# Deformable attention on one core: the weighted sum of the values as matmuls with matrices of weights, for both images at once

## The chip, the cores and the metric

The kernel runs on one core of a Trainium2 chip. The metric is the device time of one execution in microseconds (us), the median over runs. An engine is named as the profile names it: PE (matmuls) and PEld (its weight loads), DVE, ACT, POOL, and SP, which issues transfers. Transfers ("DMA") run on 16 DMA engines that all queues share; a queue belongs to the engine that issues (SP, ACT or POOL).

## The reference, cut to what matters

The program computes two layers on two images of 64 x 64 pixels with 256 channels: a deformable attention, a graph-attention mixture of experts, a windowed attention and a second mixture of experts. The change touches only the first, whose core is this, for 8 groups `g` of 32 channels and 9 sample points each:

```python
qkv = _dwconv_nhwc(x @ qkv_w + qkv_b, dw_w, dw_b)            # 1x1 and depthwise 3x3
for g in range(G):                                           # G = 8 groups, HC = 32 channels
    off = conv(q)[g] + base[g]                               # base: the 9 points of a 3x3 raster, spacing r = 2g + 1
    k_list.append(_flow_warp(k_map[:, sl], off) * mask)      # bilinear samples at y + off_y, x + off_x, clipped to the image
    v_list.append(_flow_warp(v_map[:, sl], off) * mask)
attn = softmax(einsum('bgpc,bgpkc->bgpk', q * HC ** -0.5, k))
out = einsum('bgpk,bgpkc->bgpc', attn, v)
return out @ proj_w + proj_b
```

`_flow_warp` reads the four pixels around a point with bilinear weights. Since the learned part of an offset is below one pixel on this data (the kernel tests it and has a gathering path for the other case, which does not run here), a point of group g lies within one pixel of its raster place. So each of the 9 points is a sum over a fixed 3 x 3 patch with "tent" weights, and the output of a pixel is a sum over 9 rows (`ky` = 0, 1, 2 of the raster times `sy` = 0, 1, 2 of the patch) of 9 pixels each (`kx`, `sx`), every one with a weight of its own: attention weight x mask x tent in y x tent in x.

## The kernel before, in words

Everything is float32. A pixel is named by image `b`, row `y` and column `x`; 128 partitions hold (b, y), both images' rows, unless said otherwise.

`static_maps` (L209 to L378) makes the maps in DRAM: normalisation and the 1x1 projection in 16 chunks (L236 to L259), the depthwise convolution of queries and values on DVE (L207) and of keys on PE (L349), the offsets (L365 to L378). The sorting of the graph's edges, which belongs to a later layer, is woven in (`edges`, L224, `next(edges)`). The query tile `q0` is cleared by one POOL memset (L276); `borders` (L309) has POOL issue 32 transfers that repeat the edge pixels of the value map `vd`, which is stored with 16 repeated rows and columns around each image. `qd` and `kd` are the query and key maps.

`static_attention` (L381) then works group by group, in the order 1, 2, ..., 7, 0. In phase n it weaves three lists of steps ("lanes") together by their relative place in each list: `group_values` of group n, `group_weights` of group n + 1, `group_dots` of group n + 2. Two phases before the first have no values. Every engine runs its instructions in the order so written.

- `group_dots` (L440): for a half of the columns and one `kx`, PE multiplies the 64 queries of a column with the 64 x 3 keys of three columns (L473, 32 channels deep, one image at a time, four column blocks of 8 on partitions 0, 32, 64, 96; two sets of PSUM buffers), ACT copies the products to a staging tile (L480, in the first two phases DVE takes half), and ACT issues the store to `dots` in DRAM (L492).
- `group_weights` (L506): SP reads the logits back, shifted by row (`pick`, L545, pieces of 128 bytes), DVE applies the tents, the softmax and the mask (L588 to L627), POOL multiplies the last tent in (L633, nine products of 128 x 576). The result `wt[ky]` holds for each (b, y) and x the 81 weights.
- `group_values` (L682): for each of the 9 shifted rows SP loads the value map, shifted by dy, into `vt` (L711; 64 partitions per transfer, up to 11.8 KB each). ACT spreads the row's weights into PSUM (L717). Then, for each `kx` and each quarter of the columns, DVE multiplies three shifted windows of values with their weights (L733, 128 x 1536), POOL adds one or two of the three products together (L740, 128 x 512), and PE adds what is left to the accumulators with an identity matrix (L746, 128 x 512). After the last row ACT copies the four accumulators out (L756) and issues their stores to `od`.

`project_out` (L772) reads `od` back by tiles of 128 pixels, transposes them on PE, multiplies by `proj_w` and adds input and bias. Later layers follow and are the same in both kernels.

## Time and profile before

| what | value |
|---|---|
| median of 10 runs | 6117.68 us (6105.75 to 6138.07) |
| profiled execution, its own time | 6120.16 us |
| span in its profile | 6118.3 us |
| maps, `static_maps` | about 0 to 985 us |
| the two phases without values | about 985 to 1232 us |
| eight phases with values (first product to last copy out) | 1232 to 3178 us |
| first accumulator copied out (L756), phase by phase | at 1593.6, 1847.0, 2103.0, 2362.5, 2625.3, 2854.6, 3070.3 and 3143.5 us |
| projection, `project_out` | about 3180 to 3300 us |

The span is the time from the first to the last instruction; the execution's own time is 1.9 us longer, and this execution is 2.5 us above the median. In a line of a group, "x2716 | 1402.0, 662" means 2716 instructions that kept the engine busy for 1402.0 us together and took 662 ns each on average; behind the next bar stands the idle time just before them and what ended it. A float32 matmul appears as two matmul instructions, each with its own weight load; a transpose appears as one. PEclk is the granted clock of PE, 1.0 being full. DMA share is the mean busy share of the 16 DMA engines.

### The profile page before, as it was taken

Reading aid. Unit: us, or ns where it says so; the run is one execution under the profiler, and the core shown is the slowest. Engines: PE = TensorE matmul, PEld = TensorE weight load, DVE = VectorE, ACT = ScalarE, POOL = GpSimd, SP = SyncE. Lnnn points to the kernel's source line nnn. Section 1 sums busy time; section 2 is a strip of 40 time slices with the busy share of each in tenths; the row PEclk is TensorE's granted clock in tenths of the full one; section 3 lists DMA queues with packets and bytes.
Section 4 is the critical chain, followed back from the end, with each engine's and each line's share of the span. In section 5 each row is a group of like instructions: output and inputs, shape, how many; then the busy total and the mean of one; then the engine's idle time right before and its main releaser. Section 6 shows DMA issues by size and latency. Waiting matters only on the chain. (4 is left out here: it accounts for less than half of the span.)

```text
span 6118.3 us, 68586 instructions
## 1 busy us (share of the span) xinstructions
PE 4977.6 (81%) x23911; PEld 2992.5 (49%) x23911; DVE 3728.1 (61%) x6085; ACT 1441.6 (24%) x2580; POOL 2270.7 (37%) x1994
## 2 busy tenths in 40 slices
PE   9999985597998988999878586089977878869993
PEld 5645784333343433343335243068853444448882
DVE  7897766375888888899955577011136555542223
ACT  3222111223333323321003000022223444412220
POOL 0000000054787877788841773700025111110016
PEclk9989986566988979899889798599987888879996
DMA  5436667534545546564243200277742000038885
GB/s 163 147 111 157 133 54 128 121 99 106 132 128 128 146 123 154 124 147 99 58 95 73 12 6 3 99 229 224 224 141 79 21 21 21 21 127 267 265 269 182
DMA packets 946767, 740.49 MB, mean 121 GB/s; under 512 B 611794, under 2 KB 833246, under 8 KB 935264
## 3 DMA queue, kind: packets, MB, share of 16 engines
q1 hardware_dynamic: 725004, 488.35, 31.9%
q10 hardware_dynamic: 185812, 167.81, 10.2%
q0 software_dynamic: 35584, 79.71, 4.4%
q8 instruction: 197, 3.23, 0.2%
q14 instruction: 170, 1.39, 0.1%
HBM read 469.87 MB, written 276.15 MB: 122 GB/s over the span
## 5 line engine op out<-in xcount | busy, mean ns | idle before, releaser
L746 PE MATMUL acc<-prod,ident 128*128 128x512 f32 x2716 | 1402.0, 662 | 154.6 <-POOL prod L740 131.5
L733 DVE TENSOR_TENSOR prod<-vt,wp 128x1536 f32<-128x1536 f32 (+1 forms) x796 | 1334.8, 1732 | 219.3 <-PE acc L746 163.3
L740 POOL TENSOR_TENSOR prod<-prod 128x512 f32<-128x512 f32 x1010 | 1307.8, 1319 | 428.7 <-DVE prod L733 402.3
L746 PEld LDWEIGHTS acc<-prod,ident 128*128 128x128 f32 x2716 | 527.7, 206 | 828.0 <-issue 555.2
L480 ACT COPY stage<-dot 128x384 f32<-128x384 f32 (+1 forms) x640 | 482.6, 840 | 1084.7 <-PE dot L473 909.0
L473 PE MATMUL dot<-kt,qt 32*64 32x192 f32 (+1 forms) x5888 | 516.4, 419 | 152.6 <-ACT stage L480 85.2
L1501 PE MATMUL ps_h<-xgT,w1t 128*128 128x256 f32 x2240 | 540.0, 388 | 31.1 <-DVE xgT L1496 24.6
L473 PEld LDWEIGHTS dot<-kt,qt 32*64 32x64 f32 x5888 | 282.2, 166 | 547.0 <-ACT stage L480 269.5
L1509 PE MATMUL ps_y<-w2t,hT 128*128 128x256 f32 x2240 | 507.4, 380 | 0.0
L1512 DVE TENSOR_TENSOR y<-ps_y,b2t 128x256 f32<-128x256 f32 x280 | 118.8, 424 | 627.2 <-PE ps_y L1509 458.2
L1501 PEld LDWEIGHTS ps_h<-xgT,w1t 128*128 128x128 f32 x2240 | 414.9, 192 | 110.2 <-DVE xgT L1496 34.3
L1509 PEld LDWEIGHTS ps_y<-w2t,hT 128*128 128x128 f32 x2240 | 426.5, 190 | 58.3
L1504 ACT ACTIVATE hT<-ps_h,b1t 128x256 f32<-128x256 f32 x560 | 259.1, 474 | 814.9 <-PE ps_h L1501 778.0
L1234 PE MATMUL ps<-oh,ol 128*128 128x512 f32 (+1 forms) x864 | 327.4, 542 | 95.1 <-DVE oh L1227 95.1
L2127 POOL DMA_INDIRECT xs<-tn,sloti x128 | 124.8, 975 | 610.5 <-DVE slot L2125 521.4
L1596 POOL DMA_INDIRECT back<-ys,back_row x128 | 124.9, 976 | 583.1 <-DVE run L2112 538.2
L207 DVE SCALAR_TENSOR_TENSOR cv<-pad,colt,cv 128x2048 f32<-128x2048 f32 x128 | 296.4, 2340 | 0.0
L1234 PEld LDWEIGHTS ps<-oh,ol 128*128 128x128 f32 x864 | 169.9, 198 | 252.3 <-issue 210.2
L349 PE MATMUL ps_k<-padk,diag 128*128 128x512 f32 x576 | 269.7, 623 | 19.6 <-ACT km L354 19.3
L1494 PE MATMUL ps_x<-ident,xg 128*128 128x128 f32 x560 | 84.9, 275 | 217.3 <-DMA xg<-xs 217.3
L1118 PE MATMUL psc<-oh,ol 128*128 128x64 bf16 x1792 | 239.1, 305 | 21.9 <-DVE oh L1116 21.9
L1118 PEld LDWEIGHTS <-ol 128*128 128x128 bf16 x1792 | 225.2, 148 | 52.8 <-issue 40.7
(392 smaller groups left out, 5968.8 us busy)
## 6 DMA issues: line engine op xcount, KB each, us to landing
w1t<-in_W SPq DMA_DIRECT2D x140, 512.0 KB
w2t<-in_W SPq DMA_DIRECT2D x140, 512.0 KB
xg<-xs SPq DMA_DIRECT2D x140, 256.0 KB
ys<-y ACTq DMA_DIRECT2D x140, 256.0 KB
kt<-kd SPq DMA_DIRECT2D x176, 160.0 KB
pr<-stage SPq DMA_DIRECT2D x16, 1584.0 KB
pad<-pr SPq DMA_DIRECT2D x16, 1122.0 KB
b2t<-in_b SPq DMA_DIRECT2D x140, 128.0 KB
```

The lines of the kernel that those rows point to most:

```text
L207: nc.vector.scalar_tensor_tensor(out, src, w, out, ALU.mult, ALU.add)
L349: nc.tensor.matmul(ps.rearrange("p a b -> p (a b)"), lhsT=diag[:, tap, :], rhs=pad[:, at : at + 8, tap % 3 : tap % 3 + W], start=(tap == 0 ...
L473: nc.tensor.matmul(ps[jj][H * b : H * b + H, i, 0 : m * H], lhsT=qt[at, i0 + i, :, b], rhs=kt[at, i0 + i : i0 + i + m, b, :], start=True, ...
L480: (nc.vector.tensor_copy if alone and jj else nc.scalar.copy)(box["d"][:, 0:m, :, x : x + 2].rearrange("p s y i -> p i (s y)"), ps[jj][:, ...
L733: nc.vector.tensor_tensor(pr[:, 0:m], win, wp[:, xh, 0:m, XQ * xq : XQ * xq + XQ].unsqueeze(3).to_broadcast([P, m, XQ, HC]), ALU.mult,)
L740: nc.gpsimd.tensor_tensor(pf[:, 0], pf[:, 0], pf[:, s], ALU.add)
L746: nc.tensor.matmul(box["a"][i].rearrange("p x c -> p (x c)"), lhsT=self.ident, rhs=pf[:, s, :], start=i not in started, stop=last,)
L1118: nc.tensor.matmul(psc, lhsT=ol[:, :, j], rhs=oh[:, :, j], start=(c1 == 0), stop=(c1 == NW - 1),)
L1234: nc.tensor.matmul(psf[:, c : c + m], lhsT=ol, rhs=ohf[:, c : c + m], start=(start and j == 0), stop=(stop and j == n - 1),)
L1501: nc.tensor.matmul(ps, lhsT=w1t[:, k, f * P : (f + 1) * P], rhs=xT[:, k, :], start=(k == 0), stop=(k == CC - 1),)
L1504: nc.scalar.activation(hT[:, f, :], ps, AF.Gelu, bias=b1t[:, f : f + 1])
L1509: nc.tensor.matmul(ps, lhsT=hT[:, f, i * P : (i + 1) * P], rhs=w2t[:, f, :], start=(f == 0), stop=(f == NF - 1),)
```

## The change

The sum over rows is rewritten as a matmul over the rows of both images. For a column x of the output, a half `h` of the columns and one `kx`, a matrix `[ (b, y source), y output ]` holds the weights; times the values of one column, `[ (b, y source), (b, channel) ]`, it gives the output column. The value tile has, for each (b, y), 32 channels in its own image's place and zeros in the other's, so one matmul sums both images without mixing them.

- **Zeros.** The matrices `wd[g]` lie in DRAM (`[H, B, 6, H, 3, XH]`: source row, image, (kx, h), output row, column shift, column). They are mostly zero. `zeros()` has POOL write them during `static_maps`, from a zero tile of 16 partitions in pieces of 1536 bytes, only inside the band of rows that a band of 16 source rows can reach (`band`): 368 transfers, 74.5 MB in all, eight in flight. `some(n, after)` issues n portions, behind a small POOL copy that waits for ACT's or DVE's current tile. 192 transfers (33.0 MB) stand ahead of the memset of `q0` on POOL.
- **Weights.** `along_x` is cut into three products of 128 x 192 per (ky, sy). Rows outside the image are added to the edge row's weights (`fold`, eight DVE operations of 128 x 576 per group, for g = 0 four), so the map needs no repeated rows. SP writes the nine weight rows onto the diagonals of `wd[g]` (`write`), in pieces of 384 bytes.
- **Values.** `value_map` loads a group's values once (two pieces), DVE copies them into `vt`, four copies a group. For each of 6 runs (h, kx) POOL issues eight transfers of 16 partitions that load the matrix into one of two tiles `mats`. PE then does 240 float32 matmuls a group (128 rows deep, 64 columns wide, up to 192 long, moving operand read with a step of 384 bytes), in pairs on the two halves of the output partitions. `clear` zeroes the accumulators by matmuls, `end` has ACT copy them out.
- **Dots.** Both images in one matmul: queries are loaded twice and masked by DVE (`own`), 64 channels deep, 128 wide, 192 long; half as many matmul instructions. Four sets of PSUM buffers instead of two; queries in one buffer instead of two; the store goes by bands of 16 rows in long runs, and `pick` reads pieces of 384 bytes.
- **Projection.** `od` is stored by channel, so `project_out` loads eight pieces of 32 partitions and needs no transposes; its matmuls take 64 pixels each.

The diff at its core:

```diff
+ORDER = list(range(1, G)) + [0]
+BAND = 16
+def band(g, y):
+    r = 2 * (g or G - 1) + 1
+    return max(0, y - r - 1) // 4 * 4, min(H, (y + BAND + r + 1 + 3) // 4 * 4)
...
@@ static_maps
+            zero = zp.tile([P, 4 * 3 * XH], F32, name="zero")
+            nc.gpsimd.memset(zero, 0.0)
+            def zeros():
+                for g in ORDER:
+                    for y in range(0, H, BAND):
+                        lo, hi = band(g, y)
+                        for b in range(B):
+                            for k in (range(6) if g else (0, 1, 4, 5)):
+                                to = wd[g][y : y + BAND, b, k, lo:hi].rearrange("y (n f) s x -> y n (f s x)", f=4)
+                                ins = nc.gpsimd.dma_start(
+                                    to, zero[0:BAND].unsqueeze(1).to_broadcast([BAND, (hi - lo) // 4, 4 * 3 * XH])
+                                )
+                            yield
+            def some(n, after=None):
+                if after is not None:
+                    nc.gpsimd.tensor_copy(tick, after)
+                for _ in range(n):
+                    next(fill, None)
...
+                    some(2, st[:, 5, 7, 1:2])
...
+                    some(3, cv[:, 0, 0:1])
...
+                some(B * G * H // BAND)
...
@@ static_attention
-                "prod": pool("atp", 8), "dram": pool("atd", 2, space=DRAM), "wp": pool("atw", 2, space=PSUM),
-                "dot": pool("ats", 2, space=PSUM), "acc": pool("ata", 1, space=PSUM),
+                "dram": pool("atd", 2, space=DRAM), "dot": pool("ats", 4, space=PSUM), "acc": pool("ata", 1, space=PSUM),
+            mats = [pools["one"].tile([P, H, 3, XH], F32, name=f"mat{i}") for i in range(2)]
+            pools["vt"] = pools["one"].tile([P, W + 2 * BORDER, B, HC], F32, name="vt")
...
@@ group_dots
+            box["q"] = qt = pools["one"].tile([P, XQ, H, B], F32, name="qt")
+            nc.vector.tensor_tensor(qf, qf, own.unsqueeze(1).to_broadcast([P, XQ * H, B]), ALU.mult)
...
+            for i in range(2):
+                for jj in range(2):
+                    at = slice(64 * jj, 64 * jj + 64)
+                    nc.tensor.matmul(
+                        ps[jj][:, i, :], lhsT=qt[at, i0 + i].rearrange("p y b -> p (y b)"),
+                        rhs=kt[at, i0 + i : i0 + i + 3, :].rearrange("p s y -> p (s y)"), start=True, stop=True,
+                    )
...
@@ group_weights
+            for sx in range(3):
+                nc.gpsimd.tensor_tensor(
+                    wt[ky][:, sy, :, 2 - sx, :], halves(t5[:, sx, 0, 3 * ky : 3 * ky + 3, :]),
+                    halves(box["wy"][:, sy]), ALU.mult,
+                )
...
+        def fold(i, to):
+            nc.vector.scalar_tensor_tensor(a, weights(i), edge[:, m : m + 1], a, ALU.mult, ALU.add)
+        def write(i):
...
+                        ins = nc.sync.dma_start(
+                            dst, weights(i)[H * b + lo : H * b + hi, k : k + n].rearrange("p k s x -> p k (s x)")
+                        )
...
@@ group_values
+        def load(n):
+            h, kx, _ = runs[n]
+            for b in range(B):
+                for y in range(0, H, BAND):
+                    lo, hi = band(g, y)
+                    nc.gpsimd.dma_start(mats[n % 2][H * b + y : H * b + y + BAND, lo:hi], wd[y : y + BAND, b, 2 * kx + h, lo:hi])
+        def add(n, j0, j1):
...
+                    for q in range(2):
+                        at = m.offset + a * XH + XQ * q + j - 2 + a
+                        nc.tensor.matmul(
+                            sums[h][64 * q : 64 * q + 64, j - 2 + a : j - 2 + c, :].rearrange("p x y -> p (x y)"),
+                            lhsT=vt[:, r + 1 + XH * h + XQ * q + j + dx].rearrange("p b c -> p (b c)"),
+                            rhs=bass.AP(m.tensor, at, [m.ap[0], [XH + 1, c - a], [3 * XH, H]]),
+                            start=False, stop=last and (j, a) == over,
+                        )
+        steps.append(value_map)
+        steps.append(lambda: load(0))
+        steps.append(lambda: load(1))
+        for n, (h, kx, dx) in enumerate(runs):
+            if n % (len(runs) // 2) == 0:
+                steps.append(lambda h=h: clear(h))
+            for j in range(0, XQ + 2, 3):
+                steps.append(lambda n=n, j=j: add(n, j, j + 3))
+            if n + 2 < len(runs):
+                steps.append(lambda n=n: load(n + 2))
+            if (n + 1) % (len(runs) // 2) == 0:
+                steps.append(lambda h=h: end(h))
```

## The prediction, made before the changed kernel ran

> **What bounds the kernel now.** I read the granted clock and span first (one core, clock 0.853), then the busy table by 40 slices, then busy times cut at the stage boundaries, then the costliest groups and the waits of the stage that changes. The sums over stages:
>
> ```profile
> core 0: us, PE busy (x) PEld busy (x) DVE busy (x) ACT busy (x) POOL busy (x), PEclk, DMA share, GB/s
> 0.00:320.00 320.00, 301.93 (x1376) 196.78 (x1377) 250.92 (x777) 94.43 (x163) 7.49 (x10) 0.94 0.47 155
> 320.00:985.00 665.00, 597.47 (x3074) 443.48 (x3073) 540.41 (x695) 107.97 (x113) 23.00 (x19) 0.91 0.60 105
> 985.00:1232.00 247.00, 135.18 (x1136) 77.41 (x1136) 112.62 (x179) 59.23 (x75) 13.85 (x18) 0.50 0.59 144
> 1232.00:1620.00 388.00, 343.10 (x1620) 147.50 (x1620) 259.77 (x188) 112.04 (x169) 232.90 (x179) 0.74 0.48 114
> 1620.00:2855.00 1235.00, 1132.02 (x5296) 475.52 (x5296) 1049.34 (x692) 381.03 (x603) 968.06 (x748) 0.89 0.55 131
> 2855.00:3180.00 325.00, 270.33 (x575) 111.35 (x568) 272.79 (x186) 21.74 (x53) 220.73 (x200) 0.92 0.34 69
> 3180.00:3300.00 120.00, 83.87 (x384) 65.45 (x384) 83.89 (x296) 26.42 (x84) 32.25 (x17) 0.88 0.60 149
> ```
>
> From 1620 to 2855 us PE is busy 92%, DVE 85%, POOL 78%, and the transfers a little over half. The three busy engines work on one chain, as the page's groups show:
>
> ```profile
> L746 PE MATMUL acc<-prod,ident 128*128 128x512 f32 x2716 | 1402.0, 662 | 154.6 <-POOL prod L740 131.5
> L733 DVE TENSOR_TENSOR prod<-vt,wp 128x1536 f32<-128x1536 f32 (+1 forms) x796 | 1334.8, 1732 | 219.3 <-PE acc L746 163.3
> L740 POOL TENSOR_TENSOR prod<-prod 128x512 f32<-128x512 f32 x1010 | 1307.8, 1319 | 428.7 <-DVE prod L733 402.3
> ```
>
> The product on DVE, the sum on POOL and the identity matmul wait for one another in turn; each alone fills two thirds of the 1946 us between the first product (1232) and the last copy out (3178). A phase lasts 252 us (first copies out at 1593.6 and 2854.6, five phases apart). The copies and reductions that remain are in the same stretch (1232 to 3180 us, shapes kept apart):
>
> ```profile
> L480 ACT COPY stage<-dot 128x384 f32<-128x384 f32 x539 | 411.1, 855 | 837.7 <-PE dot L473 719.5 <-DMA dots<-stage 53.1 <-PE acc L746 21.9
> L756 ACT COPY o<-acc 128x512 f32<-128x512 f32 x32 | 18.8, 587 | 115.7 <-PE acc L746 48.7 <-DMA lk<-dots 33.0 <-DMA od<-o 19.8
> ...
> L613 DVE TENSOR_REDUCE red<-lg 128x64 f32<-128x576 f32 x7 | 8.0, 1143 | 0.2
> L612 DVE TENSOR_TENSOR lg<-lg,mask 128x576 f32<-128x576 f32 x7 | 5.5, 785 | 0.2
> ```
>
> L480 writes with a step of 128 bytes and takes 2.2 ns an element, L756 without a step 1.15; L613 reads with a step of 256 bytes and takes 2.0 ns, L612 without 1.36. A step costs up to a factor of two.
>
> **The change, per phase of groups 1 to 7.** What goes: L733, L740, L746 and the spreading copy L717 (73.3 us on ACT): 1335 us of DVE, 1308 of POOL and 1402 of PE. What then sets the phase? I bill every engine.
>
> PE. Dots: 48 steps a group. A step was 16 instructions, of which four ran side by side, in 0.87 to 0.88 us at full clock (timeline near 1612 us); now it is 8, two side by side, so again four rounds of 192 columns: 48 x 0.87 = 42 us. Values: 36,864 columns on two halves that run side by side as the dots' tiles do, so 18,432, in two instructions, at 0.84 ns (a round of 192 columns started 162 ns after the last): 31 us if the step of 384 bytes is free, 62 us at the factor of two above, 124 us if the two halves also share the reads. I take 62, the nearest row. Clearing: 4 matmuls of 512 columns, 4 us. Sum 108 us (79 to 170); PE is in order, so a late matrix also holds the dots behind it.
>
> ACT. 96 copies x 0.855 = 82 us (the step becomes 384 bytes; L480 already pays), 24 stores at 0.82 us of issuing = 20, copies out and tents 10: 112 us.
>
> DVE. All but L733 and L480 is 240 us in seven phases, 34 us each; eight folds at 0.8 (128 x 576), two masks of 2048 elements at 2.4 (twice the 1.22 us of 128x1024), four value copies of at most 1.7, smaller pieces 2: 54 us. POOL: 27 products at a third of 1.5 us, 16 us, and 48 issues at 0.5 to 1.15 us (the border transfers): 40 to 71 us. SP: about 118 transfers at 0.52 to 0.62 us: 68 us. None of these binds.
>
> Transfers, in us of all 16 engines, from the packets in the trace: dots stores 9.1 MB at 16.8 bytes/ns (5632 bytes in 336 ns) 34; keys 768 x 4608 bytes 13; queries, twice as many, 7; values, loaded once, 4 (before: nine loads, 48); logits read and weights written, 6912 pieces each at 23 ns (256 bytes took 18, 512 took 27) 20; offsets and output 6. That is 84. The matrices, 9.5 MB, come by 16 partitions, which no row shows: 27 us at the rate of a 128-partition load (8976 bytes in 410 ns), 35 at that of the 32-partition dots stores, and at most 108 if a quarter of the first rate is left, since 64-partition value loads had already dropped to 11,776 bytes in 844 ns. I take 50, between the two nearer values because 16 partitions are fewer than any row. Sum 134 (111 to 192). The busiest slices of the page show 8 tenths; at 0.84 the phase is 134 / 0.84 = 160 us. This is the largest bill, so **160 us a phase**, 132 to 256 at the ends (192 at 0.75).
>
> [...]
>
> Waits between phases. The first matrix of a group waits for the last products (POOL), folds (DVE), 12 writes (SP, behind whose waits the next keys queue) and their landing: 3 x 0.6 + 4 x 0.8 + 12 x 0.55 + about 5 = 17 us, then the load. POOL issues these last products after the load that waits for run 3 of 6, so two runs of PE, some 50 us, cover it. Without that cover it would cost 17 to 30 us a phase.
>
> Group 0 has four runs and no dots beside them: 4 x 18 us of load and matmul and 18 us to the end, 90 us, against 110 before.
>
> Stage: 7 x 160 + 90 = 1210 instead of 1946: **-736 us**.
>
> **The rest.** Zeros: 74.5 MB in 48,512 pieces of 1536 bytes beside the maps. Before, 0 to 985 us holds 549 us of all DMA engines (0.47 x 320 + 0.60 x 665). At 70 ns a piece (between 1024 bytes at 54 and 2048 at 97) the zeros add 212: 761 of 985, hidden, with PE at 90% setting the pace. At a quarter of that rate they add 850, and the maps grow by up to 414 us. On POOL 368 issues cost under 420 us, off the path, but the clearing of q0 (at 324.5 us before) now follows 192 of them, 33 MB: ACT's copies into q0, and after two tiles DVE, wait for it. I take +40 (0 to +250, since the engines seldom stand on the same pieces). The two phases without values: PE no longer waits for single PSUM pairs, but the weights of group 1 still follow dots, softmax and now writes and a load: 0 (-60 to +20). Projection: 128 transposes go (20.6 us), yet all eight loads and the input (16.8 MB, 67 us at 250 GB/s) stand before the first matmul, where before they ran beside: +15 (-15 to +60).
>
> Sum on the profiled execution's 6120: 6120 - 736 + 40 + 15 = 5439, **5440 us**; the median, 2.5 us lower, makes no difference to that.
>
> **The rivals.** Written by T, the time of a phase: 6120 - 1946 + 90 + 55 + 7T = 4319 + 7T.
>
> - All transfers at their low ends. T = 111 / 0.84 = 132, with ACT's 112 and PE's 108 just below: 5243 us. For it: 32-partition loads run at 17 bytes/ns. Against: three engines near the same bill seldom overlap fully.
> - The matmuls become the bound: the two halves share the strided reads, and dots run at the 0.74 clock of 1232 to 1620 us: 124 + 57 + 4 = 185, with waits for matrices 200: 5719 us. For it: ACT's and DVE's rows at half rate. Against: the dots' tiles lose nothing side by side.
> - Slower: transfers by 16 partitions run at a quarter. T = 256, the maps +250 instead of +40: 4319 + 1792 + 210 = 6321 us. It decides where T passes 257 with cheap zeros, or 227 with dear ones. For it: the drop from 128 to 64 partitions. [...]
>
> **How the numbers follow.** Forecast (5300 to 5650) 0.53, first rival 0.17, second 0.22, slower one 0.06; the rest, 0.02, is a wait between phases that cancels the gain or leaves no change. The range runs from below the first rival to above the second, 5190 to 5780, and leaves out a little under 2 in 10. Under 0.2% either way (about what this measurement can tell) is next to impossible between such values: 0.01. Faster 0.92, slower 0.07.
>
> **What would show it.** Right: L733, L740, L717 gone; first copies out 140 to 190 us apart; DMA share 0.75 or more there, with DVE and POOL under half. The value matmuls at about 320 ns instead of 160 a round show the step's price; 640 the second rival. Matrix loads much longer than 20 us, with PE waiting for them, show the 16-partition price. A q0 memset far after 324 us, or the start of dots far after 985 us, shows the zeros' cost. The prediction is wrong if phases stay above 230 us or the maps grow by more than 200.

## The result and the profile after

The changed kernel takes 6321.14 us (median of 8 runs, 6307.59 to 6336.02) where the kernel before takes 6119.88 (28 runs): 1.0329 times as long, 95% interval 1.0318 to 1.0341. The forecast was 5440, range 5190 to 5780. It is slower by 201 us, and the forecast had the wrong sign.

The two profiled executions have spans of 6308.2 and 6118.3 us, 189.9 apart. Cut at the same four events (first dots matmul, first instruction on values, last copy out, end) they give the whole difference:

| stretch | before, us | after, us | difference | forecast |
|---|---|---|---|---|
| maps: 0 to the first dots matmul | 995.0 | 1680.3 | +685.3 | +40 (0 to +250) |
| dots and weights alone, to the first instruction on values | 237.4 | 238.5 | +1.1 | 0 |
| stage with values, to the end of the last copy out | 1946.3 | 1431.6 | -514.7 | -736 |
| the rest | 2939.6 | 2957.8 | +18.2 | +15 |

This is the table of busy times of the changed kernel, in stretches that end with the chunk loop (739), the first dots matmul (1680.3), the first value matmul (1918.8) and the last copy out (3350.4):

```profile
core 0: us, PE busy (x) PEld busy (x) DVE busy (x) ACT busy (x) POOL busy (x), PEclk, DMA share, GB/s
0.00:739.00 739.00, 492.01 (x2482) 345.01 (x2482) 511.46 (x1403) 93.08 (x162) 104.03 (x197) 0.72 0.58 106
739.00:1680.30 941.30, 463.69 (x1984) 307.00 (x1985) 317.90 (x146) 107.13 (x114) 156.46 (x229) 0.74 0.89 127
1680.30:1918.80 238.50, 115.70 (x742) 97.52 (x742) 115.31 (x146) 72.54 (x92) 26.24 (x44) 0.68 0.49 128
1918.80:3350.40 1431.60, 886.41 (x5949) 601.29 (x5948) 308.68 (x382) 408.87 (x589) 304.02 (x565) 0.78 0.75 150
3350.40:6308.20 2957.80, 2177.86 (x10969) 1534.51 (x10969) 1237.42 (x3371) 642.63 (x1344) 801.30 (x823) 0.84 0.41 121
```

The chunk loop ended at 289 us before and ends at 739. Through it PE is busy 67% of the time (94% in the first 320 us before), DVE 69% and the DMA engines 58%: nothing is full. From 739 to 1680 the share is 0.89. In the stage with values, where PE, DVE and POOL were all busy before, PE is down to 62%, ACT to 29%, DVE to 22%, POOL to 21%, and the DMA engines stand at 0.75. So the old bound is gone, and none of the bills has taken its place in full.

The page's groups, which answer to the three (L746, L733, L740) and to L480 of before:

```profile
L534 PE MATMUL dot<-kt,qt 64*128 64x192 f32 x2944 | 473.5, 417 | 646.5 <-DVE qt L518 240.9
...
L541 ACT COPY stage<-dot 128x384 f32<-128x384 f32 x640 | 444.6, 853 | 861.8 <-PE dot L534 466.0
L847 PE MATMUL acc<-mat,vt 128*64 128x192 f32 (+2 forms) x3680 | 499.7, 439 | 121.9 <-DMA mat<-wd 121.9
...
L825 POOL DMA_DIRECT2D mat<-wd x368 | 179.7, 494 | 911.0 <-PE acc L847 533.4
...
L259 POOL DMA_DIRECT2D wd<-zero x368 | 197.3, 540 | 347.3 <-DMA wd<-zero 330.0
```

The value matmuls (L847) cost 500 us where product, sum and identity matmul cost 1335, 1308 and 1402 on their three engines. A copy of dots costs 853 ns, 855 before. New are 911 us in which GpSimd waits at L825 ahead of a matrix load, 533 of them for value matmuls to leave a buffer, and 330 us in which it waits for earlier zeros before it can issue more (L259).

What holds the chunk loop shows in the waits from its 45th us to its end (columns: total us, times, longest), first of the changed kernel, then of the kernel before:

```profile
engine line waited for: us in total, times, longest us
POOL tick L272 <- ACT stage L306: 528.8, 14, 62.5
ACT stage L306 <- PE ps_q L302: 248.7, 70, 24.1
ACT stage L306 <- DMA pr<-stage: 245.5, 7, 45.2
```

```profile
ACT stage L255 <- PE ps_q L251: 154.5, 89, 6.4
```

Before, ACT's copies into the staging buffer waited only for PE, at most 6.4 us at a time. Now they wait seven times, up to 45 us and 245 in all, for the store of a chunk to leave the buffer that they want to refill; they also wait 94 us more for PE. The store hasn't changed: 1584 KB in packets of 2112 bytes, whose median is 88 ns. What is new beside it are the zeros' packets: 14,208 of 4608 bytes, median 739 ns, 6.2 bytes/ns. All the zeros' packets add up to 717 us of all 16 engines.

At the end the dots wait for the zeros themselves. The last offset copy starts at 1531.7 us (954.1 before), and PE then stands from 1564.3 to 1680.3, until DVE has masked the queries:

```profile
DVE qt L518 <- DMA mask<-offd: 87.2, 1, 87.2
```

The view names the loads of the sample mask, but these are issued only at 1675.9, behind the load of `edge` (L449), which holds the mask for the queries. SyncE stands from 1600.2 to 1675.4 before it issues that load, and the profile puts this down to the zeros, whose last packet ends at 1674.9. So 578 of the 685 us lie ahead of the last offset copy, and some 75 of the rest are a plain wait for the last zero.

In the stage the copies out end at 2034.6, 2300.7, 2488.3, 2705.5, 2914.7, 3141.9, 3273.3 and 3350.4 us, one group each: 188 to 266 us apart while dots run beside, 131 for group 7, 77 for group 0, on the average (3273.3 - 1918.8) / 7 = 193.5 us instead of 160.

### The profile page after: what moved, and what is told of

Same layout as the page of the kernel before. It is cut to its first block, busy times and chain, and to the rows that moved or that the text cites. A ratio compares the mean times of both kernels' runs of the same rounds, so it can differ in the third digit from the quotient of the medians.

```text
span 6308.2 us, 63605 instructions
## 1 busy us (share of the span) xinstructions
PE 4135.7 (66%) x22123; PEld 2885.3 (46%) x22123; DVE 2490.8 (39%) x5448; ACT 1324.2 (21%) x2300; POOL 1392.0 (22%) x1856
## 5 line engine op out<-in xcount | busy, mean ns | idle before, releaser
L534 PE MATMUL dot<-kt,qt 64*128 64x192 f32 x2944 | 473.5, 417 | 646.5 <-DVE qt L518 240.9
L534 PEld LDWEIGHTS dot<-kt,qt 64*128 64x128 f32 x2944 | 378.1, 233 | 751.0 <-issue 523.0
L541 ACT COPY stage<-dot 128x384 f32<-128x384 f32 x640 | 444.6, 853 | 861.8 <-PE dot L534 466.0
L847 PE MATMUL acc<-mat,vt 128*64 128x192 f32 (+2 forms) x3680 | 499.7, 439 | 121.9 <-DMA mat<-wd 121.9
L847 PEld LDWEIGHTS acc<-mat,vt 128*64 128x64 f32 x3680 | 309.1, 159 | 309.0 <-issue 225.9
L825 POOL DMA_DIRECT2D mat<-wd x368 | 179.7, 494 | 911.0 <-PE acc L847 533.4
L302 PE MATMUL ps_q<-xT,wq 128*128 128x512 f32 x384 | 225.7, 730 | 106.5 <-ACT stage L306 94.7
L259 POOL DMA_DIRECT2D wd<-zero x368 | 197.3, 540 | 347.3 <-DMA wd<-zero 330.0
L395 PEld LDWEIGHTS ps_k<-padk,diag 128*128 128x128 f32 x576 | 114.5, 202 | 336.3 <-issue 211.5
## 6 DMA issues: line engine op xcount, KB each, us to landing
mat<-wd POOLq DMA_DIRECT2D x112, 192.0 KB, 12.4
```

The costliest lines, as they stand in the source:

```text
L259: ins = nc.gpsimd.dma_start(to, zero[0:BAND].unsqueeze(1).to_broadcast([BAND, (hi - lo) // 4, 4 * 3 * XH]))
L302: nc.tensor.matmul(ps.rearrange("p a b -> p (a b)"), lhsT=wq[:, k, c * P : (c + 1) * P], rhs=xT[:, k, :], start=(k == 0), stop=(k == CC - 1),)
L395: nc.tensor.matmul(ps.rearrange("p a b -> p (a b)"), lhsT=diag[:, tap, :], rhs=pad[:, at : at + 8, tap % 3 : tap % 3 + W], start=(tap == 0 ...
L534: nc.tensor.matmul(ps[jj][:, i, :], lhsT=qt[at, i0 + i].rearrange("p y b -> p (y b)"), rhs=kt[at, i0 + i : i0 + i + 3, :].rearrange("p s y ...
L541: (nc.vector.tensor_copy if alone and jj else nc.scalar.copy)(box["d"][:, :, :, x : x + 2].rearrange("p y s i -> p i s y"), ps[jj].rearran ...
L847: nc.tensor.matmul(sums[h][64 * q : 64 * q + 64, j - 2 + a : j - 2 + c, :].rearrange("p x y -> p (x y)"), lhsT=vt[:, r + 1 + XH * h + XQ * ...
```

## The experiments

Two questions: what made the maps 685 us longer, and why a phase takes 194 instead of 160 us. For the first, theory A is the 16-partition source of the zeros, theory B their place in GpSimd's order, theory C its queue. For the second, theory M (transfers set the phase) stands against W (waits in a chain), and later S (SyncE's in-order queue).

Experiments 9 to 12, 17 and 18 ran on two chips where the kernel before takes 6116 to 6118 us, the others on three where it takes 6400 to 6411, so ratios are to the kernel before on the same chip. The 280 us between these chips lie behind the last copy out (2954 to 2963 us there on the first two, 3238 to 3252 on the other three); where an edit left the maps alone they end at the same time on all, so lengths of maps and stage can be compared across.

### 1. Zeros from 96 partitions

```
-  for b in range(B):
-      for k in (range(6) if g else (0, 1, 4, 5)):
-          to = wd[g][y : y + BAND, b, k, lo:hi] ...            # from zero[0:BAND]
+  for h in range(2):
+      to = wd[g][y + 8 * h : y + 8 * h + 8, :, :, lo:hi].rearrange("y b k (n f) s x -> (y b k) n (f s x)", f=4)
+      nc.gpsimd.dma_start(to, zero[0:96] ...)
```

> The changed kernel, but each strip's zeros leave 96 partitions in two transfers instead of 16 partitions in twelve; same queue, same places in GpSimd's order, 3.9 MB more (group 0 gets all six blocks). Theory A (the 16-partition source is slow, 4608 bytes in 739 ns, and other transfers wait behind its packets): packets of 4608 bytes fall to 180-290 ns, the zeros' engine time from 23% of the span to under 10%, the first dots matmul comes at 1000-1150 us instead of 1680, total 5640-5790. Theory B (the zeros' place in GpSimd's order holds up the sort and the clearing of q0): the maps keep most of their 685 us, total 6100-6300.

Measured: 0.9585 of before (0.9557 to 0.9613). The table of busy times up to the end of the chunk loop, to the first dots matmul, and in the stage:

```profile
core 0: us, PE busy (x) PEld busy (x) DVE busy (x) ACT busy (x) POOL busy (x), PEclk, DMA share, GB/s
0.00:493.00 493.00, 315.40 (x1262) 192.09 (x1262) 241.40 (x753) 92.65 (x162) 60.53 (x86) 0.74 0.74 224
493.00:1232.10 739.10, 608.04 (x3216) 454.61 (x3214) 586.88 (x796) 108.18 (x114) 47.94 (x35) 0.87 0.63 122
...
1467.80:2891.70 1423.90, 889.24 (x5949) 606.78 (x5948) 308.48 (x382) 408.35 (x589) 307.06 (x565) 0.78 0.75 151
```

The first dots matmul comes at 1232.1 instead of 1680.3, 448 us earlier, and the stage is as before (1424 instead of 1432). The packets of 4608 bytes fall from a median of 739 ns to 178 (mean 254), the zeros' engine time from 717 to 271 us. Of the 448 us, 335 lie ahead of the last offset copy (1531.7 to 1197.1) and 113 behind it, since the last zero now lands at 553 and nothing waits for it. One thing in the expectation doesn't hold: a step of the filling now covers both images, so all strips, not half, are issued beside the chunks (the DMA rate there is 224 GB/s). Theory A gets most of the loss, but less than it said (dots at 1000 to 1150); 237 us remain. The edit also makes 64 transfers out of 368; experiment 4, which changes the partitions of a load and not the number of loads, shows that the partitions alone can make packets shorter (12288 bytes in 834 ns instead of 1362).

### 2. The same zeros issued by SyncE

```
-  ins = nc.gpsimd.dma_start(to, zero[0:BAND] ...)
+  ins = nc.sync.dma_start(to, zero[0:BAND] ...)
```

> The changed kernel, with the same 368 transfers of zeros from 16 partitions issued by SyncE instead of GpSimd. Theory A: the packets stay at 739 ns, the maps stay within 100 us of 1680, total 6200-6450. Theory B, or a theory C (GpSimd's software queue itself is slow): packets at 200-300 ns or a chunk loop that ends near 290 us, total 5650-5900.

Measured: 1.0859 (1.0837 to 1.0882). The table (columns as before) up to the end of the chunk loop and to the first dots matmul:

```profile
0.00:627.00 627.00, 303.50 (x1088) 177.51 (x1089) 204.73 (x621) 96.67 (x162) 11.95 (x26) 0.70 0.63 115
627.00:2033.50 1406.50, 633.05 (x3387) 478.37 (x3386) 630.97 (x929) 109.91 (x114) 39.67 (x30) 0.66 0.57 88
```

The rate stays: 1536 bytes in 232 ns is 6.6 bytes/ns, and the packets add up to 634 us. The maps take 353 us longer still, against the 100 expected. The chunk loop ends earlier than in the changed kernel (627 for 739), but the convolution of the keys comes later: its loads stand behind the zeros in SyncE's queue. The last zeros are issued at 1630.8 and the first of these loads at 1632.8 (788.3 in the changed kernel); the convolution runs from 1641 to 1897 us (804 to 1324). Theory C falls. So does B for the clearing of q0: without zeros on GpSimd it comes 47 us after the chunk loop; in the changed kernel it comes 51 after it, before the change 36. The loop is late, not the clearing.

### 3. Two buffers for the queries

```
-  qt = pools["one"].tile(...)           # and raw of 48 columns, o of 16
+  qt = pools["first"].tile(...)         # two buffers; raw of 12 columns, o of 4 to make room
```

> The changed kernel with two buffers for the queries qt instead of one (room comes from value_map in pieces of 12 columns and copies out in quarters). Theory W (a phase of some 205 us is a chain of waits, and PE, ACT and GpSimd all stand while the one qt is filled and masked, two gaps of 25 to 30 us a phase): first copies out 150-175 us apart, total 6030-6130. Theory M (the transfers set the phase): under 60 us gained, total 6260-6330.

Measured: 1.0529 (1.0512 to 1.0547), the stage 1575 us instead of 1432. This says nothing on the queries alone: the values now come in up to eight pieces through one small buffer, and DVE waits 108 us for these pieces. Experiment 7 asks the question without that.

### 4. Rows on every fourth partition

```
-  nc.gpsimd.dma_start(mats[n % 2][H * b + y : H * b + y + BAND, lo:hi], wd[...])
+  nc.gpsimd.dma_start(mats[n % 2][H * b + y // BAND : H * b + H : H // BAND, lo:hi], wd[...])
```

> The changed kernel with the rows of a strip laid on every fourth partition of 64 instead of on 16 neighbours, for the matrices and the values alike, so that each matrix load reaches 64 partitions' width with the same bytes (the values come in eight loads instead of one). Theory M (matrix packets of 12288 bytes at 1336 ns set the phase): packets near 700 ns, phases 170-180 us, total 6080-6170. Theory W: packets fall, but the phase stays within 10 us of 205, total 6250-6330.

Measured: 1.0129 (1.0103 to 1.0155), 1.9% below the changed kernel. Over the stage the median packet of 12288 bytes falls from 1362 to 834 ns, that of 18432 from 2328 to 1361. The stage (columns as before):

```profile
1921.00:3240.10 1319.10, 898.83 (x5949) 604.77 (x5948) 313.00 (x382) 408.70 (x589) 301.24 (x565) 0.80 0.67 163
```

It is 1319 us long, 113 less, at a DMA share of 0.67. That lies between the two forecasts, so it decided nothing by itself.

### 5. The wide zeros, spread

```
-  some(2, st[:, 5, 7, 1:2])
+  if i8 % 2:
+      some(1, st[:, 5, 7, 1:2])
```

> The zeros of the first experiment (96 partitions, two transfers a strip), but spread: one strip after every second chunk and three after each tile of values, so that 8 of 32 strips lie beside the chunks instead of all 32. If the first experiment's remaining 237 us (dots at 1232 instead of 995) are its 64.7 MB crowded beside the chunks, the chunk loop ends at 295-350 us, the first dots matmul comes at 1010-1090, ratio to the kernel before 0.92-0.945. If zeros cost their bytes wherever they lie, the dots stay at 1180 or later and the ratio at 0.95-0.96.

Measured: 0.9598 (0.9575 to 0.9622), the same as experiment 1. The chunk loop ends at 401 us instead of 493 and the last offset copy comes at 1111 instead of 1198, but the dots at 1209. The edit did less than it says: a zero transfer doesn't depend on the copy that paces it, and in GpSimd's order transfers stand ahead of these copies (12 of 64 before the first), so some 53 of 78 MB still moved before 400 us.

### 6. Spread zeros, every fourth partition, two query buffers

```
-  qt = pools["one"].tile(...)           # values through raw and nc.vector.tensor_copy
+  qt = pools["first"].tile(...)
+  nc.gpsimd.dma_start(vt[H * b + y // BAND : H * b + H : H // BAND, 0:wb, b, :], vd[g, b, y : y + BAND, ...])
```

> The experiment before it, with every strip's rows on each fourth partition (as in the fourth experiment, both images' loads in turn), two buffers for the queries, the values loaded by GpSimd straight into vt (no raw tile, no copies on VectorE) and the copies out in halves. Theory M (transfers set the phase): the fourth experiment's 112 us of the stage and little more, ratio 0.90-0.925. Theory W (the waits for queries and values stand in the chain as well): phases of 150-180 us, 150 us more, ratio 0.875-0.90.

Measured: 0.9413 (0.9392 to 0.9434), outside both ranges: the maps take 1179 us instead of the 1010 to 1090 on which both counted, and the stage 1343, more than with experiment 4 alone. Two query buffers with values that GpSimd writes straight into vt bring nothing.

### 7. Half the queries' refills left out

```
   def queries(h):
+      if h:
+          return
```

> The changed kernel without the second half's queries (the first half's, already masked, are used again, so the second half's dot products are left out of the reference's sum), which takes away one of the two refills of qt a phase and nothing else. Theory W: each refill stops PE, ACT and the matrix loads for 25-40 us, so 7 x 25-40 = 175-280 us less than the changed kernel, ratio to the kernel before 0.99-1.006. Theory M: under 60 us less, ratio 1.023-1.033.

Measured: 1.0268 (1.0248 to 1.0288), 0.6% or some 39 us below the changed kernel, the stage 1406. That is M's side: the refill of qt in the middle of a phase is worth 4 to 6 us. In the changed kernel PE shows gaps of 4 to 14 us at these refills; those at a phase's start, with gaps of up to 28 us, stayed, and no run leaves them out.

### 8. Value matmuls that read neighbours

```
-  rhs=bass.AP(m.tensor, at, [m.ap[0], [XH + 1, c - a], [3 * XH, H]])
+  rhs=bass.AP(m.tensor, at, [m.ap[0], [H, c - a], [1, H]])
```

> The changed kernel with the value matmuls reading 64 to 192 neighbouring elements instead of elements 384 bytes apart (the sums are then over other weights, so the attention's output is left wrong); instructions, columns and waits are the same. If the step doubles a value matmul, as the prediction had it, L847 falls from 500 to 250-300 us of busy time. If PE is on the path, the ratio falls by that share, to 0.995-1.012; if transfers or waits set the phase it stays at 1.02-1.035. If L847 stays at 450-500, the step costs nothing.

Measured: 1.0336 (1.0317 to 1.0356), no difference. The group of the value matmuls of 192 columns, shapes kept apart, in the changed kernel and in this one (total us, mean ns):

```profile
L847 PE MATMUL acc<-mat,vt 128*64 128x192 f32 x2208 | 390.2, 502 | 0.0
```

```profile
L847 PE MATMUL acc<-mat,vt 128*64 128x192 f32 x2208 | 239.1, 364 | 0.0
```

The mean length of an instruction falls from 502 to 364 ns, but instructions overlap, so that is not the price. In the changed kernel a round of 192 columns (an instruction on each half) starts 325 ns after the last, in this one 163 (medians over the stage): the step of 384 bytes doubles a round, as the prediction had it. The busy time of L847 falls from 500 to 301 us, at the edge of what was expected for a doubling. And it gains nothing: PE isn't on the path.

### 9. Zeros for one group of eight

```
-  for g in ORDER:                        # zeros into wd[g]; matrices read wd[g]
+  for g in [G - 1]:                      # zeros into wd[G], a ninth tile; matrices read wd[G]
```

> Zeros for one group instead of eight (11.8 MB from 96 partitions into a tile of its own, where every group's matrix loads now read; the weights are still written, but nobody reads them, so the attention's output is left wrong). So far each us of engine time that zeros added (719 us in the changed kernel, 283 in the first experiment) put the first dots matmul off by 0.84 to 0.95 us. Theory M (the maps wait for transfers, even at a DMA share of 0.6): 11.8 MB are some 40 us of engine time, first dots matmul at 1025-1050 us. If ticks and order on GpSimd cost something of their own: 1090 or later. In the stage no load waits for weights to land: theory W then gives phases 20 us or more below 205, theory M within 10 us.

Measured: 0.9334 (0.9312 to 0.9356). The last offset copy starts at 970.8 us, 17 after the 954.1 of before, with 40 us of zeros. The first dots matmul comes only at 1070.8, between the two forecasts. In the last stretch ahead of it (965 to 1075 us) PE and GpSimd wait for this:

```profile
PE dot L533 <- DVE qt L517: 63.2, 1, 63.2
POOL topa L1263 <- DVE top L1261: 50.5, 1, 50.5
```

The dots now wait for the mask on qt, an instruction of DVE that the change adds, and DVE is in the middle of the edge sort then; SyncE, too, issues the loads of the queries only behind the sort's, at 1061. That is a wait of about 60 us which the late zeros of the changed kernel had hidden. The stage doesn't test W cleanly: values of a group start before its weights, its gaps are 216 to 225 us with dots beside, none shorter.

### 10. Spread zeros and every fourth partition

```
   # the edits of experiments 5 and 4, and:
-  for b in range(B):
-      for y in range(0, H, BAND):        # matrix loads
+  for y in range(0, H, BAND):
+      for b in range(B):
```

> The wide, spread zeros of the fifth experiment with the rows on every fourth partition and both images' loads in turn; one qt and the values as in the changed kernel. The two gains added up (447 + 112 to 130 us): ratio 0.936-0.946. If two buffers for the queries were worth what taking away half the refills was (40 us): 0.946-0.952.

Measured: 0.9342 (0.9308 to 0.9376). Maps 1239, stage 1302: the two gains add up, and the edits of experiment 6 beyond these had only cost.

### 11. No matrix loads

```
   def load(n):
+      if g > 1:
+          return
```

> The changed kernel with the matrices of groups 2 to 7 not loaded (groups 2 to 7 use what groups 1 left, so the attention's output is left wrong); matmuls, weights, zeros and everything else stay. The loads are 54 us of engine time a phase (162.8 us in three phases), 326 us in six. Theory M: 0.8-0.95 us of time for each, so 260-310 us less than the changed kernel, ratio 0.985-0.993. Theory W (waits for queries, keys and weights in turn): under 120 us less, ratio above 1.014.

Measured: 1.0134 (1.0107 to 1.0160), 1.9% or some 119 us below the changed kernel. The stage (columns as before):

```profile
1923.80:3237.60 1313.80, 873.60 (x5949) 636.42 (x5948) 312.91 (x382) 405.90 (x589) 170.62 (x277) 0.81 0.49 118
```

This settles it against M. The DMA share falls from 0.75 to 0.49, the stage only from 1432 to 1314 us; the five gaps between groups' ends that were 221 us on the average are 189, with no matrix loaded at all, and the last two grow from 208 to 251. M asked for 260 to 310 us; W's forecast (under 120 us, ratio above 1.014) is met in the time and just missed in the ratio. Nearly all of it comes from the first gap, 266 to 125 us; the four behind it add up to 821 instead of 841. And at the six starts of a group without loads the first value matmul now follows the last one of the group before within 4 us, where 28 to 103 us passed in the changed kernel. So neither the loads' engine time nor the wait for a group's first matrix makes a phase as long as it is; what this run leaves are the dots, the weights and the order on the queues. Experiment 4, which only spread the loads, had gained as much as leaving them out.

### 12. The weights' products on VectorE

```
-  nc.gpsimd.tensor_tensor(wt[ky][:, sy, :, 2 - sx, :], ...)
+  (nc.gpsimd if near else nc.vector).tensor_tensor(wt[ky][:, sy, :, 2 - sx, :], ...)
```

> The changed kernel with the weights' products (along_x, L705) of groups 1 to 7 on VectorE instead of GpSimd, where they stand behind matrix loads that wait for PE (533 us in all). Theory W (this wait is carried into the weights, their writes and the next matrices): 80 us or more less, ratio under 1.021. Theory M: within 30 us, ratio 1.028-1.038.

Measured: 1.0259 (1.0234 to 1.0283), 0.7% below the changed kernel and between the two forecasts; the stage is 1411, 21 us shorter. So taking the products from behind 533 us of GpSimd's waits gains 20 to 40 us.

What is left is SyncE's queue. Its instructions in one phase of the changed kernel, from the timeline (start, length, line, transfer, how many):

```profile
2547.32 14.95 SPq L625 DMA_DIRECT2D lk<-dots  x14
2566.65 2.19 SPq L525 DMA_DIRECT2D kt<-kd  x4
2568.95 28.81 SPq L625 DMA_DIRECT2D lk<-dots  x18
2597.86 3.56 SPq L525 DMA_DIRECT2D kt<-kd  x8
...
2627.36 28.04 SPq L745 DMA_DIRECT2D wd<-wt  x8
2655.69 2.51 SPq L525 DMA_DIRECT2D kt<-kd  x4
```

Reads of logits, keys, values and writes of weights go through one queue in order. The 18 reads at 2568.95 take 28.81 us with their waits, and the keys for the next dots go out behind them, at 2597.86. Of the 28.04 us of writes at 2627.36, one write of 53 rows by 6 pieces takes 12.4 us and another in the same phase 11.1; the median write takes 0.54. Over the four phases to 2914.7 SyncE issues for 96 us a phase, 38 of them writes.

### 13 to 16. SyncE's queue

Each is experiment 10 with the values kept in DRAM in the order of the partitions, so that they come in one load (13); 14 to 16 add one edit each:

```
-  ins = nc.sync.dma_start(dst, weights(i)[...])                  # 14
+  ins = nc.gpsimd.dma_start(dst, weights(i)[...])
+  cut = lo + (hi - lo) // 16 * 16                                # 15: rows lo..cut and cut..hi
-  nc.sync.dma_start(qt[p0 : p0 + HC], ...)                       # 16, and kt
+  nc.scalar.dma_start(qt[p0 : p0 + HC], ...)
```

> The tenth experiment with the values kept in DRAM in the order of the partitions, so that they come in one load on SyncE again instead of eight (18 us of issuing a phase become 2). Theory S (SyncE's in-order queue sets the phase): 7 x 8-16 us less than the tenth experiment (ratio 0.9342), 0.915-0.926. If the queue doesn't set it: 0.931-0.938.

Measured: 0.9324 (0.9303 to 0.9345), stage 1269. Below what S asked for.

> The thirteenth experiment with the weights written by GpSimd instead of SyncE (38 us of issuing a phase leave SyncE, 27 issues of about 0.5 us come to GpSimd). Theory S: 20-38 us a phase less than in the thirteenth, 140-260 us, ratio lower by 0.023-0.043. If the queue doesn't set the phase: within 0.006 of the thirteenth, or slower by what GpSimd's waits for PE cost.

Measured: 0.9331 (0.9301 to 0.9361), stage 1264. Nothing, with SyncE's writes gone; the same writes now stand behind GpSimd's own waits.

> The thirteenth experiment with each weight write cut in two, a multiple of 16 rows and the rest, so that no long write has an odd number of rows. Writes of 53 rows took 11 to 12 us of SyncE; if that is what the odd count costs, the writes' issuing falls from 38 to 15-25 us a phase in spite of more of them. Theory S: 10-20 us a phase less, ratio lower by 0.011-0.023. Otherwise within 0.005.

Measured: 0.9233 (0.9208 to 0.9257), stage 1230. The line of the writes in the changed kernel and, one number on, in this one (lengths on SyncE: least, median, most):

```profile
L745 SPq DMA_DIRECT2D wd<-wt x170: 218/538/12377, 1830.9 to 3267.8; - x170
```

```profile
L747 SPq DMA_DIRECT2D wd<-wt x294: 231/403/2360, 1389.7 to 2629.6; - x147
```

The longest write falls from 12.4 to 2.4 us. 38 us of the stage go and 20 of the stretch ahead of it. The first gap between two groups' ends shrinks by 43; the others change by -6 to +4. That is real, but experiment 14 had freed SyncE as well and gained nothing. So SyncE's time alone doesn't explain it; experiment 14 kept the uneven writes themselves, and whether it is their late landing that counted, or GpSimd's waits took back what SyncE gave, no run shows. Behind the first gap neither matters.

> The thirteenth experiment with queries and keys loaded by ScalarE's queue instead of SyncE's, so that they no longer stand behind logit reads that wait for stores and behind weight writes (20 us of issuing a phase and their waits for PE go along). Theory S: 20-40 us a phase less, ratio lower by 0.023-0.046. Otherwise, or if ScalarE's copies now stand behind those waits instead: within 0.006 or slower.

Measured: 0.9370 (0.9336 to 0.9403), stage 1278. The gaps between groups' ends add up to 1087 us instead of 1153, but the first group ends 428 us after the first dots instead of 354: what the gaps gave, the start took back. S doesn't set the phase either.

### 17 and 18. Later keys by ScalarE, and values by GpSimd

```
-  nc.sync.dma_start(kt[p0 : p0 + HC], ...)                                 # 17, and qt, on experiment 15
+  (nc.sync if alone else nc.scalar).dma_start(kt[p0 : p0 + HC], ...)
-  nc.vector.tensor_copy(vt[H * b : H * b + H, x : x + n, b, :], ...)       # 18, on 17
+  nc.gpsimd.tensor_copy(vt[H * b : H * b + H, x : x + n, b, :], ...)
```

> The fifteenth experiment (ratio 0.9233) with queries and keys loaded by ScalarE's queue except in the first phase, where dot products run alone. If keys standing behind the logit reads in SyncE's queue are a link of each phase's chain, the gaps between groups' ends shorten by some 8-12 us each and the start stays as in the fifteenth: 50-75 us, ratio 0.911-0.916. If the gain of the sixteenth was only the start's loss moved: 0.920-0.926.

Measured: 0.9215 (0.9192 to 0.9239), stage 1222; not told apart from experiment 15. The gaps add up to 37 us less than there, and the first group ends 32 us later behind the first dots: again the start takes back what the gaps give.

What 18 takes away shows in DVE's timeline of the changed kernel, the copies of the next values and the last folds behind them:

```profile
2672.58 1.92 DVE L818 COPY vt<-raw 64x1536 f32<-64x1536 f32 x2 [37.75 <-PE acc L847]
2674.53 3.38 DVE L728 SCALAR_TENSOR_TENSOR wt<-wt,edge 128x576 f32<-128x576 f32 x4
```

The folds stand behind a copy that waited 37.75 us for value matmuls. PE's timeline shows the start of an earlier group, the last value matmuls at 2476 and the next at 2538, and below it the mask that the dots at 2524.71 follow, in DVE's timeline:

```profile
2476.61 10.64 PE L847 MATMUL acc<-mat,vt 128*64 128x64 f32 x80
...
2494.95 1.98 PE L830 MATMUL acc<-cstt,none 128*128 128x512 f32 x4
2524.71 5.73 PE L534 MATMUL dot<-kt,qt 64*128 64x192 f32 x34 [27.78 <-DMA tents<-offd]
...
2534.47 3.66 PE L534 MATMUL dot<-kt,qt 64*128 64x192 f32 x16 [0.75 <-ACT stage L541]
2538.06 16.56 PE L847 MATMUL acc<-mat,vt 128*64 128x64 f32 x126
```

```profile
2522.32 2.29 DVE L518 TENSOR_TENSOR qt<-qt,edge 128x2048 f32<-128x2048 f32 x1 [42.15 <-DMA qt<-qd]
```

Here PE stands 27.78 us until the next queries are loaded and masked, and then runs dots before it comes to the value matmuls.

> The seventeenth experiment with the copies of the values into vt on GpSimd instead of VectorE, so that the last four folds and the writes behind them no longer wait for the last value matmuls. If that is the link between one group's end and the next group's first matrix (35-50 us without value matmuls at each start), 10-25 us a phase go, ratio 0.010-0.025 below the seventeenth. If not: within 0.004.

Measured: 0.9190 (0.9161 to 0.9220), 5621 us where the kernel before takes 6118: the fastest of all, though not told apart from 17. That is the "if not": at the starts of groups 2 to 7 still 36 to 60 us pass without a value matmul (22 to 63 in experiment 17), so the folds' place isn't the link. The table (columns as before) up to the first dots matmul and in the stage:

```profile
0.00:1213.50 1213.50, 924.40 (x4474) 649.41 (x4474) 833.78 (x1555) 204.64 (x277) 102.16 (x112) 0.83 0.68 167
...
1436.40:2647.10 1210.70, 880.46 (x5949) 597.55 (x5948) 296.63 (x352) 410.37 (x586) 341.17 (x593) 0.82 0.71 176
```

| run | ratio to before | maps, us | stage, us |
|---|---|---|---|
| changed kernel | 1.0329 | 1680 | 1432 |
| 1 zeros from 96 partitions | 0.9585 | 1232 | 1424 |
| 2 zeros by SyncE | 1.0859 | 2033 | 1436 |
| 4 every fourth partition | 1.0129 | 1682 | 1319 |
| 7 half the refills | 1.0268 | 1678 | 1406 |
| 8 neighbours | 1.0336 | 1674 | 1461 |
| 10 spread zeros, every fourth | 0.9342 | 1239 | 1302 |
| 11 no matrix loads | 1.0134 | 1679 | 1314 |
| 12 products on VectorE | 1.0259 | 1682 | 1411 |
| 13 values in one load | 0.9324 | 1230 | 1269 |
| 15 writes by 16 rows | 0.9233 | 1239 | 1230 |
| 18 all of it | 0.9190 | 1214 | 1211 |

## Why the prediction was wrong

**Zeros, +40 (0 to +250): the step that turned the sign.** Two choices in it failed. The first is the price of a piece: 70 ns for 1536 bytes, from rows of 128 partitions, with the quarter rate kept for a bound "since the engines seldom stand on the same pieces"; how often they do, no run shows. The trace has 739 ns for 4608 bytes, a third of it (246) for each 1536: 717 us of engine time instead of 212. Experiment 1 shows the cause, the same zeros from 96 partitions at 178 ns and the dots 448 us earlier. The second is the cover. The step added engine time up to a share of 1 (761 or, at the quarter rate, 1399 of 985 us), as if whatever the maps leave idle could be filled. The last offset copy moved by 578 us for 717 of zeros, by 243 for 271 (experiment 1), by 156 for 272 (experiment 5), by 17 for 40 (experiment 9). That DMA engines are only 47% to 60% busy didn't hide the transfers: the maps wait for stores and loads of their own in turn, and these waits grew: ACT's for its chunk stores from none to 245 us, DVE's for the loads of `pad` (L227) from none to 364, ACT's for the stores of the value map (L351, before L299) from 47 to 214. That their packets stand behind zeros on the same engines is an inference; the waits of ACT for its own store show it only from outside. A third cost had no term at all: the dots wait some 75 us for the last zero to land. So the high end had to be 700 and not 250.

The clearing of q0 was said to follow 192 transfers. It does, at 789.9 us, but only 51 us behind the chunk loop; the loop itself was late, which the step didn't consider.

**The phase, 160 us: the bills were nearly right, and the rule from bills to time was not.** Three phases from 2300.7 to 2914.7 us hold a share of 0.78 of 614 us, 159 us a phase, against 134. Matrices took 54 (forecast 50), dots stores 40 (34), the small pieces of logits and weights 29 (20), keys 15 (13). PE and ACT never came near their limit, as forecast. What failed is "at 0.84 the phase is 134 / 0.84": a share read from the busiest slices of the page was made a law, and the largest bill the bound. Experiment 11 took 54 us from that bill in each of six phases and 118 us from the whole stage, some 20 a phase and most of it in the first, and the share fell to 0.49. Experiments 7, 8, 12, 14 and 16 took away a refill, two fifths of the value matmuls' time, GpSimd's waits, SyncE's writes and its keys, and got 26, no, 21, 5 and no us of the stage. So none of these bounds the phase by itself. What is left is a chain: dots, weights and values of three groups run in one order on five in-order queues and hand on one another's waits. That is a conclusion from what fell, not a run's result; which links make up the 155 to 201 us of a gap that stay in experiment 18 isn't settled.

**Waits between phases, said to be covered.** They aren't: 51 us pass without a value matmul between 2487 and 2538, 28 to 103 at each start of groups 2 to 7. The step counted products, folds, writes and a load, 17 us and the load, and put them under two runs of PE. It missed that folds stand on DVE behind copies that wait for these very runs, and that PE first waits for the next queries (27.78 us of the 51). Moving the copies alone (experiment 18) brought 11 us of the stage, within the measurement. And without loads (experiment 11) these gaps close while the stage gains only 118 us, so most of the wait lies beside another chain.

**SyncE, 68 us, "none of these binds".** It was 96, since single writes took up to 12.4 us. Of the writes of 6 pieces a row (L745), those of 53, 59, 61 and 62 rows, four of each, took 5.8, 3.8, 3.4 and 6.1 us in the median and up to 12.4, 8.4, 6.7 and 10.5, while the 14 of 64 rows took 0.64 and up to 1.7. Two of the four of 53 rows took only 0.2 and 0.4 us, so the rows alone don't set the time. Cut at multiples of 16 rows (experiment 15), the longest took 2.4 us, and 0.9% of the kernel before went; what makes a write long, no run shows. That SyncE doesn't bind held.

**What held.** L733, L740, L746 and L717 went, and no engine that they bound is left above 62%. The stretch without values stayed (+1 for 0), the rest grew by 18 (15 forecast). Group 0 took 77 us (90). The factor for the matmuls' step, 2, held (325 ns a round against 163, experiment 8), and the value matmuls took 65 us a group (62).

**The rivals.** The slower one named 16-partition transfers, the right cause, and its 6321 us is the measured median; that is chance. It had phases of 256 us and maps of +250; measured were 194 and +685. Matrices ran at 8 to 13 bytes/ns and zeros, all from the same 16 partitions, at 6.2, a quarter of the 25.9 from 96 (experiment 1). That the eight strips of a matrix lie on different partitions may be why they ran faster; no run tests it by itself. The point from which it decides was put at 227 us a phase with dear zeros; with zeros as dear as they are it is 165 (4319 + 645 + 7T = 6120). The same formula with the measured 194 gives 6322.

## What to carry to other kernels

Price a transfer by its own shape, its partitions first: 16 neighbouring partitions as the source ran at a quarter of the rate of 96 (6.2 against 25.9 bytes/ns) and cost 448 us, which turned a gain of some 250 us (experiment 1) into a loss of 200. Don't fill idle DMA time on paper: in these maps, which wait for their own transfers in turn, each us of engine time added cost 0.4 to 0.9 us, at shares of 0.47 to 0.60 before. When a bound is removed and no bill comes near the time that is left, forecast the chain of waits, not the largest bill. Price a pipelined instruction by the time from one start to the next, not by its length: a round of value matmuls started every 325 ns, while an instruction lasted 502.

## What was not expected of the hardware

Zeros issued by SyncE moved at the same rate as by GpSimd (6.6 against 6.2 bytes/ns), yet made the maps 353 us longer, as the keys' loads then stood behind them in the same queue. Loads to every fourth partition of 64 gained as much as no loads at all (113 and 118 us of the stage). Two of the four weight writes of 53 rows held SyncE for 11.1 and 12.4 us, the other two for 0.2 and 0.4; taking the weight writes off SyncE gained nothing while cutting their rows at multiples of 16 gained 0.9%.
